# A graph network on one core: constants and scores of the gathering passes held in PSUM, small copies on ACT, and one bias matmul for three

## The chip, the core and the metric

The kernel runs on one NeuronCore of a Trainium2 chip. Its engines work side by side and meet only through semaphores: PE (TensorE, matrix products), ACT (ScalarE, functions and copies), DVE (VectorE, elementwise work), POOL (GpSimd, here mostly the issue of indirect gathers), and SP (SyncE, which issues the other DMAs). SBUF holds operands; PSUM, in banks of 2 KB per partition, holds what PE accumulates. The metric is the device time of one execution in microseconds; less is better.

## What is computed

A graph with 3125 nodes of 128 features and 100,000 edges, which come sorted by their destination `dst`, goes through four blocks, each applied to the relu of a layer norm of the node features `x` and added to them. The part that matters, in short:

```python
# block 1: three attention layers of the GAT kind over (src, dst)
# block 2: a message layer
m   = gelu(concat(h[dst], h[src], edge_attr) @ W1 + b1)
m   = gelu(m @ W2 + b2) @ W3 + b3
agg = segment_mean(m, dst)            # then an update of the node
# block 3: two layers of dynamic attention, 4 heads of 32 features
e     = leaky_relu(xl[src] + xr[dst], 0.2)
score = einsum('ehd,hd->eh', e, att)
mx    = segment_max(score, dst)
ex    = exp(score - mx[dst])
den   = segment_sum(ex, dst)
out   = segment_sum(ex / den[dst] * xl[src], dst)
# block 4: two convolution layers
out   = segment_sum(dinv[src] * edge_weight * dinv[dst] * (h @ W)[src], dst)
```

`segment_sum` adds the rows of all edges with the same destination.

## The kernel before

The nodes stand in 25 tiles of 128. The first block works densely: the number of edges between each pair of nodes is counted, and attention is taken over whole tiles. The other five passes (one message layer, two attention layers, two convolutions) are **gathering passes** over the edges. A plan cuts the sorted edges into 30 windows, each of which adds to one node tile; together they have 840 columns of 128 edges, in 220 chunks of at most four columns. Every gathering pass loops over windows, and inside over chunks.

`gather` (L1226) lets GpSimd issue one indirect DMA for each column: 128 rows of a table in HBM, chosen by `src`, land in SBUF as `g`. The message layer and the convolution have six such chunk buffers (`g1`), the attention layers 22 (`g2`), since they keep a window's rows until its scores are done.

Two one-hot matrices carry edges to nodes and back. `node_by_slot` (L1237) compares a row of node numbers, fetched by an SP DMA in bf16, with `pidx`, the number of the partition: `at`, nodes by edges. `slot_by_node` (L1242) compares `iota_row`, the numbers 0 to 127 along a row, with the local destination `dst_l`: `w`, edges by nodes. A segment sum is then a matmul of `w` with the rows, which accumulates in PSUM over all columns of a node tile. Every PSUM tile comes from one pool with two buffers for each name, `bank(name)`, each a whole bank; the accumulator is `bank("C")`, so that successive node tiles use two different banks.

In the message layer, for each chunk: the edge attributes are transposed on PE and copied out by DVE (`ets`, L1321); `by_feature` puts the sum of three bf16 parts of the destination's product times `at` (L1249), the edge part (L1332) and the transposed gathered rows (L1254) into one bank; ACT takes the gelu `x1` (L1338). Three bias matmuls with one row each (L1342) and four products with W2 (L1346) follow, the second gelu `x2` on ACT (L1349), a column of ones by GpSimd (L1351), the edge weights by DVE (L1352), and the accumulation (L1355).

In an attention layer, for each chunk of a window: `by_feature`; ACT and DVE take the leaky relu `low_y` (L1528, L1529); PE multiplies with the attention vector (L1532), and ACT copies the scores into `S` (L1534), a tile in SBUF. After the window, `run_maxima` finds the maximum of each run of edges with one destination by two scans along the columns and two along the partitions (L1455 to L1480); DVE subtracts it (L1538) and ACT takes the exponential (L1539). A second loop over the window's chunks multiplies the rows by it (`msg`, L1545), copies it beside them on ACT (L1548), builds `w` and accumulates (L1551).

In a convolution, for each column, `w` is compared and multiplied by the edge weight in one DVE instruction (L1603), and two passes of PE accumulate it (L1605).

Tiles are shared out by the framework, which sets a semaphore wait wherever an instruction touches what another engine's instruction still uses, and which lays the instructions of the loops out ahead of each other where buffers allow. Each engine then runs its own queue in order.

Of the kernel before, what the change touches and what calls it, by code (L numbers as in the profile page):

```python
# [18 lines left out]
P = 128  # L19
# [725 lines left out]
def sorted_path(ctx: ExitStack, tc: tile.TileContext, a: dict, out: bass.AP, flag_out: bass.AP):  # L745
# [20 lines left out]
    ps = ctx.enter_context(tc.tile_pool(name="f_ps", bufs=2, space=PSUM))  # L766
# [5 lines left out]
    def bank(name):  # L772
        return ps.tile([P, SL], F32, name=name)
# [118 lines left out]

    with tc.tile_pool(name="f_prep", bufs=1) as pp:
# [84 lines left out]
    wgt = ew_pool.tile([P, KT], F32, name="wgt")  # L978
# [6 lines left out]
    def load_edge_windows(pool):  # L985
        raw = pool.tile([P, KT], I32, name="raw", bufs=1)
        lo_r = pool.tile([P, KT], F32, name="lo_r", bufs=1)
        hi_r = pool.tile([P, KT], F32, name="hi_r", bufs=1)
        t_r = pool.tile([P, KT], F32, name="t_r", bufs=1)
        for i, (lo, hi, t, c0, k) in enumerate(plan.ew):  # L990
            cs = slice(c0, c0 + k)
            r = at_register(base_e, i, P * k)
            nc.sync.dma_start(src_i[:, cs], window_of(a["src"], r, k))
            nc.sync.dma_start(wgt[:, cs], window_of(a["edge_weight"], r, k))
            reads.append(nc.sync.dma_start(raw[:, cs], window_of(a["dst"], r, k)))
            nc.gpsimd.memset(lo_r[:, cs], float(lo))
            nc.gpsimd.memset(hi_r[:, cs], float(hi))
            nc.gpsimd.memset(t_r[:, cs], float(t * P))
        nc.vector.tensor_copy(dst_w, raw)

        nc.vector.tensor_tensor(lo_r, dst_w, lo_r, ALU.is_lt)
        nc.vector.tensor_tensor(hi_r, dst_w, hi_r, ALU.is_ge)
        nc.vector.tensor_add(lo_r, lo_r, hi_r)
        nc.vector.tensor_sub(dst_l, dst_w, t_r)
        nc.vector.scalar_tensor_tensor(dst_l, lo_r, FAR, dst_l, ALU.mult, ALU.add)
# [206 lines left out]
    for c0 in range(0, KT, P):  # L1212
        n = min(P, KT - c0)
        pt = bank("D")
        nc.tensor.transpose(pt[:n, :P], dst_l[:, c0:c0 + n], ident)
        t = wk.tile([P, P], BF16, name="place")
        nc.vector.tensor_copy(t[:n, :], pt[:n, :P])
        nc.sync.dma_start(place_d[c0:c0 + n, :], t[:n, :])

# [10 lines left out]
    def node_by_slot(c0, n):  # L1230

        row = wk.tile([P, SL], BF16, name="row", bufs=4)
        nc.sync.dma_start(row[:, :n * P], bass.AP(tensor=place_d.tensor,
                                                  offset=place_d.offset + c0 * P,
                                                  ap=[[0, P], [1, n * P]]))
        at = wk.tile([P, SL], BF16, name="at", bufs=3)
        nc.vector.tensor_scalar(at[:, :n * P], row[:, :n * P], pidx, None, ALU.is_equal)  # L1237
        return at

    def slot_by_node(c0, n):  # L1240
        w = wk.tile([P, C, P], F32, name="w", bufs=3)
        nc.vector.tensor_tensor(w[:, :n, :], bc(iota_row[:, None, :], [P, n, P]),  # L1242
                                bc(dst_l[:, c0:c0 + n, None], [P, n, P]), ALU.is_equal)
        return w
# [16 lines left out]
    def message_layer(H):  # L1261
# [8 lines left out]
        b2 = load_row("mb2", a["L1_gnn_mb2"], parts=1)  # L1270
# [9 lines left out]
        b2_3 = thirds(b2, "b2_", gp, D)  # L1280
# [8 lines left out]
        R3 = thirds(R, "R_", big, NT * D, "Z")  # L1289
        sums = big.tile([P, NT, D], F32, name="T")  # L1290
# [3 lines left out]
        for i, (lo, hi, t, w0, k) in enumerate(plan.ew):  # L1294
            if i == first_of[t]:
                acc = bank("C")
            r = at_register(base_e, i, P * k)
            ea = a["edge_attr_64"][bass.ds(r, P * k), :].rearrange("(p k) f -> p k f", p=P)
            for c0, n in chunks_of(w0, k):
# [10 lines left out]
                at = node_by_slot(c0, n)  # L1310

                et = bank("A")
# [28 lines left out]
                for q in range(3):  # L1341
                    nc.tensor.matmul(y2[:, :n * P], ones_bf[0:1, :],  # L1342
                                     bc(b2_3[q][:, None, :], [1, n, D]),
                                     start=(q == 0), stop=False, skip_group_check=True)
# [6 lines left out]
                nc.gpsimd.memset(x2[:, :n, D:D + 1], 1.0)  # L1351
                nc.vector.tensor_copy(x2[:, :n, D + 1:W], wgt[:, c0:c0 + n, None])  # L1352
                w = slot_by_node(c0, n)
# [38 lines left out]

    def find_runs(pool, keep):

        fwd = keep.tile([P, HEADS, KR], BF16, name="fwd")
        bwd = keep.tile([P, HEADS, KR], BF16, name="bwd")
# [15 lines left out]
        for h in range(HEADS):  # L1412
            nc.vector.tensor_scalar(fwd[:, h, :], one, -BIG, None, ALU.mult)
            nc.vector.tensor_scalar(bwd[:, h, :], other, -BIG, None, ALU.mult)
# [25 lines left out]

    def run_maxima(i, k, S):

        fwd = wk.tile([P, HEADS, k + 2], BF16, name="fw")
        bwd = wk.tile([P, HEADS, k + 2], BF16, name="bw")
        nc.vector.tensor_copy(fwd, breaks["fwd"][:, :, off[i]:off[i] + k + 2])
        nc.vector.tensor_copy(bwd, breaks["bwd"][:, :, off[i]:off[i] + k + 2])
# [5 lines left out]
        B = wk.tile([P, HEADS, k + 2], F32, name="B")  # L1452

        def scan():
            nc.vector.tensor_tensor_scan(flat(F), flat(fwd), flat(S), -BIG, ALU.add, ALU.max)  # L1455
            nc.vector.tensor_tensor_scan(flat(B)[:, ::-1], flat(bwd)[:, ::-1], flat(S)[:, ::-1], -BIG,
                                         ALU.add, ALU.max)
# [3 lines left out]
        pt = bank("D")  # L1461
        nc.tensor.matmul(pt[:HEADS, 0:P], F[:, :, k], ident, start=True, stop=True)
        nc.tensor.matmul(pt[:HEADS, P:2 * P], B[:, :, 1], ident, start=True, stop=True)
        edge = wk.tile([HEADS, 2 * P], F32, name="edge")
        nc.vector.tensor_copy(edge, pt[:HEADS, :2 * P])
# [3 lines left out]
        nc.vector.tensor_tensor_scan(run[:, 0, 1:], lane[:, :P], edge[:, :P], -BIG, ALU.add, ALU.max)  # L1469
        nc.vector.tensor_tensor_scan(run[:, 1, P - 1::-1], lane[:, :P - 1:-1], edge[:, :P - 1:-1], -BIG,  # L1470
                                     ALU.add, ALU.max)
        pt = bank("D")
# [11 lines left out]
    def dynamic_attention_layer(H, i_layer):  # L1484
# [13 lines left out]
        for h in range(HEADS):  # L1498
# [3 lines left out]
        HT = transposed(H, big.tile([P, NP], F32, name="T"))  # L1502
        T = big.tile([P, NT, D], F32, name="YT")
        product(HT, Wl, lambda t0, n, pt: nc.vector.tensor_add(
            T[:, t0:t0 + n, :], pt, bc(bl[:, None, :], [P, n, D])))
# [4 lines left out]
            bc(br[:, None, :], [P, n, D])))  # L1510
        R3 = thirds(R, "R_", big, NT * D, "T")
        Y = big.tile([P, NT, D], F32, name="Z")

        for i, (lo, hi, t, w0, k) in enumerate(plan.ew):
            if i == first_of[t]:
                acc = bank("C")
            gs = []
            S = wk.tile([P, HEADS, k + 2], F32, name="S")
            for c0, n in chunks_of(w0, k):
                j0 = c0 - w0  # L1520
                g = gp.tile([P, C, D], F32, name="g2", bufs=22)
                gs.append(g)
                gather(tab, g, 0, c0, n)
                at = node_by_slot(c0, n)
                y1 = bank("A")
                by_feature(y1, R3, t, at, g, 0, n)
                low_y = wk.tile([P, SL], F32, name="low_y", bufs=3)
                nc.scalar.mul(low_y[:, :n * P], y1[:, :n * P], SLOPE)  # L1528
                nc.vector.tensor_max(low_y[:, :n * P], y1[:, :n * P], low_y[:, :n * P])  # L1529
                sp = bank("B")  # L1530
                for c in range(n):
                    nc.tensor.matmul(sp[:, c * HEADS:(c + 1) * HEADS], low_y[:, c * P:(c + 1) * P], att_h,  # L1532
                                     start=True, stop=True)
                nc.scalar.copy(S[:, :, 1 + j0:1 + j0 + n].rearrange("p h c -> p c h"),  # L1534
                               sp[:, :n * HEADS].rearrange("p (c h) -> p c h", h=HEADS))
            M = run_maxima(i, k, S)
            ex = wk.tile([P, k, HEADS], F32, name="ex")
            nc.vector.tensor_sub(S[:, :, 1:k + 1], S[:, :, 1:k + 1], M[:, :, 1:k + 1])  # L1538
            nc.scalar.activation(ex.rearrange("p k h -> p h k"), S[:, :, 1:k + 1], AF.Exp)  # L1539
            for c0, n in chunks_of(w0, k):  # L1540
# [8 lines left out]
                w = slot_by_node(c0, n)  # L1549
# [25 lines left out]
    def convolution_layers(H):  # L1575
# [7 lines left out]
        for i_layer in (1, 2):  # L1583
# [9 lines left out]
            Y = big.tile([P, NT, D], F32, name="Z")  # L1593
            for i, (lo, hi, t, w0, k) in enumerate(plan.ew):
                if i == first_of[t]:
                    acc = bank("C")
                for c0, n in chunks_of(w0, k):
# [3 lines left out]
                    for c in range(n):  # L1601
                        j = c0 + c
                        nc.vector.tensor_scalar(w[:, c, :], iota_row, dst_l[:, j:j + 1], wgt[:, j:j + 1],  # L1603
# [17 lines left out]
    with tc.tile_pool(name="f_big1", bufs=1) as big, tc.tile_pool(name="f_w1", bufs=1) as wt, \  # L1621
            tc.tile_pool(name="f_g1", bufs=2) as gp:
        weights.append(wt)
        into_x(message_layer(prenorm("H")))
    with tc.tile_pool(name="f_big2", bufs=1) as big, tc.tile_pool(name="f_w2", bufs=1) as wt:
        weights.append(wt)
        with tc.tile_pool(name="f_runs", bufs=1) as rp:
            find_runs(rp, wt)
        h = prenorm("YT")
        with tc.tile_pool(name="f_g2", bufs=2) as gp:  # L1630
# [3 lines left out]
    with tc.tile_pool(name="f_big3", bufs=1) as big, tc.tile_pool(name="f_w3", bufs=1) as wt, \  # L1634
            tc.tile_pool(name="f_g3", bufs=2) as gp:
# [47 lines left out]
```

## Time and profile before

| what | value |
|---|---|
| median of 3 runs | 8938.41 us (8935.47 to 8966.12) |
| the profiled execution | 8952.42 us, span 8950.6 us |
| PE busy | 5047.8 us (56%) |
| weight loads (PEld) busy | 3996.2 us (45%) |
| DVE busy | 3410.2 us (38%) |
| ACT busy | 1265.6 us (14%) |
| POOL busy | 4110.5 us (46%) |

The profile is of one execution. Every engine's busy time is a share of the whole span, averaged over stages that differ; these can be told apart in the slices of the page:

```profile
PE   4677769999964455555635555555533333333332
...
POOL 1000036666624544444344444444266666566664
PEclk9999989999986677666666676666655555555555
```

Each digit is a fortieth of the span (224 us) in tenths. GpSimd becomes busy where the gathering passes begin: the message layer from about 1230 us, the attention layers from 2736 and 4590, the convolutions from 6457 and 7707. PEclk is the clock granted to PE.

### The profile page before, as it was taken

To read this page: it belongs to the slowest core of one execution; us is meant where nothing else is said; L and a number is where in the kernel's file an instruction comes from. 1 tells how busy PE (TensorE), PEld (TensorE's weight loads), DVE (VectorE), ACT (ScalarE), POOL (GpSimd) and SP (SyncE) were. 2 spreads that over 40 slices of the span, in tenths; PEclk is the share of its full clock that TensorE was granted. 3 is DMA by queue.
4 is the path that set the end of the run, shared out by engine and by line. 5 is a ranking of instruction groups with operands and counts; after the bars stand their busy time and mean duration, and the time that the engine had idled before them with its cause. 6 is when DMAs were issued, how large, how long until landed. Compare 5 with 4: busy or idle time off the path is not lost. (4 is left out here: it accounts for less than half of the span.)

```text
span 8950.6 us, 84054 instructions
## 1 busy us (share of the span) xinstructions
PE 5047.8 (56%) x28459; PEld 3996.2 (45%) x28744; DVE 3410.2 (38%) x8010; ACT 1265.6 (14%) x2766; POOL 4110.5 (46%) x5004
## 2 busy tenths in 40 slices
PE   4677769999964455555635555555533333333332
PEld 1267756666653444445534454444422332223222
DVE  8999942222243233333343333333522112212112
ACT  1644422222210011111101111111100000000000
POOL 1000036666624544444344444444266666566664
PEclk9999989999986677666666676666655555555555
DMA  1000022323211111111111111111111111111111
GB/s 26 7 3 1 1 59 84 84 84 84 81 40 48 49 48 50 46 47 47 44 42 45 48 49 46 48 46 48 31 45 47 46 46 46 44 45 47 46 46 41
DMA packets 311528, 411.33 MB, mean 46 GB/s; under 512 B 126095, under 2 KB 235070, under 8 KB 311093
## 3 DMA queue, kind: packets, MB, share of 16 engines
q0 software_dynamic: 134560, 276.34, 11.0%
q1 hardware_dynamic: 167379, 123.47, 5.1%
q10 hardware_dynamic: 9154, 6.03, 0.3%
q8 instruction: 236, 3.87, 0.2%
q14 instruction: 199, 1.63, 0.1%
HBM read 395.06 MB, written 10.44 MB: 45 GB/s over the span
## 5 line engine op out<-in xcount | busy, mean ns | idle before, releaser
L1226 POOL DMA_INDIRECT g<-tab,src_i x4200 | 4055.0, 965 | 3507.2 <-issue 1759.9
L1605 PE MATMUL C<-g,w 128*128 128x128 f32 x3360 | 897.1, 421 | 1513.7 <-issue 709.6
L1605 PEld LDWEIGHTS C<-g,w 128*128 128x128 f32 x3360 | 709.3, 298 | 1701.4 <-issue 1184.7
L1603 DVE TENSOR_SCALAR w<-iota_row,dst_l,wgt 128x128 f32<-128x128 f32 x1680 | 467.6, 361 | 1790.7 <-remote 1242.3
L1532 PE MATMUL B<-att_h,low_y 128*128 128x4 f32 x3360 | 541.4, 282 | 872.3 <-DVE low_y L1529 579.1
L1532 PEld LDWEIGHTS B<-att_h,low_y 128*128 128x128 f32 x3360 | 547.1, 244 | 911.4 <-DVE low_y L1529 604.0
L1254 PE MATMUL A<-ident,g 128*128 128x128 f32 x3360 | 672.7, 336 | 178.5 <-issue 165.2
L1254 PEld LDWEIGHTS A<-ident,g 128*128 128x128 f32 x3360 | 610.1, 243 | 279.2 <-issue 221.0
L1551 PE MATMUL C<-msg,w 128*128 128x132 f32 x3360 | 490.0, 301 | 410.5 <-DVE w L1242 206.4
L1551 PEld LDWEIGHTS C<-msg,w 128*128 128x128 f32 x3360 | 456.0, 210 | 439.2 <-issue 348.5
L1242 DVE TENSOR_TENSOR w<-iota_row,dst_l 128x512 f32<-128x512 f32 (+2 forms) x660 | 436.4, 664 | 524.8 <-remote 185.8
L1529 DVE TENSOR_TENSOR low_y<-A,low_y 128x512 f32<-128x512 f32 (+3 forms) x440 | 289.6, 662 | 680.2 <-ACT low_y L1528 484.8
L1249 PE MATMUL A<-at,R 128*128 128x512 bf16 (+3 forms) x1141 | 444.5, 461 | 79.1 <-issue 49.1
L1545 DVE TENSOR_TENSOR msg<-g,ex 128x512 f32<-128x512 f32 (+3 forms) x440 | 284.5, 669 | 523.2 <-issue 462.4
L1351 POOL MEMSET x<- 128x4 f32 (+1 forms) x220 | 26.6, 121 | 947.8 <-issue 929.8
L1528 ACT ACTIVATE low_y<-A 128x512 f32<-128x512 f32 (+3 forms) x440 | 252.3, 578 | 1378.7 <-remote 763.0
L1237 DVE TENSOR_SCALAR at<-row,pidx 128x512 bf16<-128x512 bf16 (+2 forms) x660 | 227.0, 349 | 452.8 <-remote 158.2
L867 ACT ACTIVATE T<-R 128x3200 f32<-128x3200 f32 x3 | 8.6, 2869 | 2492.1 <-DVE R L866 2492.1
L1321 DVE COPY ets<-A 128x256 f32<-128x256 f32 (+1 forms) x214 | 88.8, 415 | 620.7 <-PE A L1316 571.7
L1249 PEld LDWEIGHTS <-R 128*128 128x128 bf16 x1980 | 224.7, 125 | 173.0 <-issue 82.8
L1155 DVE SCALAR_TENSOR_TENSOR p<-up,s_src,dn 128x1024 f32<-128x1024 f32 (+1 forms) x225 | 294.2, 1321 | 4.0 <-PE C L1161 3.6
L1157 ACT ACTIVATE p<-p 128x1024 f32<-128x1024 f32 (+1 forms) x225 | 245.2, 1092 | 299.3 <-DVE p L1155 290.0
(350 smaller groups left out, 6688.0 us busy)
## 6 DMA issues: line engine op xcount, KB each, us to landing
row<-place_d SPq DMA_DIRECT2D x597, 128.0 KB
g<-tab,src_i POOLq DMA_INDIRECT x4200
er<-in_edge_attr_dram SPq DMA_DIRECT2D x39, 512.0 KB
tab<-T SPq DMA_DIRECT2D x3, 1600.0 KB
tab<-YT SPq DMA_DIRECT2D x2, 1600.0 KB
row<-place_d SPq DMA_DIRECT2D x24, 96.0 KB
out_dram<-X SPq DMA_DIRECT2D x1, 1536.0 KB
row<-place_d SPq DMA_DIRECT2D x21, 64.0 KB
```

Of the source, the lines that this page charges most:

```text
L1155: nc.vector.scalar_tensor_tensor(p[:, :n], up[:, :n], s_src[:, st:st + 1], dn[:, :n], ALU.add, ALU.max)
L1226: nc.gpsimd.indirect_dma_start(out=g[:, j0 + c, :], out_offset=None, in_=tab, in_offset=bass.IndirectOffsetOnAxis(ap=src_i[:, c0 + c:c0 + ...
L1242: nc.vector.tensor_tensor(w[:, :n, :], bc(iota_row[:, None, :], [P, n, P]), bc(dst_l[:, c0:c0 + n, None], [P, n, P]), ALU.is_equal)
L1249: nc.tensor.matmul(pt[:, :n * P], R3[i][:, t * D:(t + 1) * D], at[:, :n * P], start=(i == 0), stop=False, skip_group_check=True)
L1254: nc.tensor.matmul(pt[:, c * P:(c + 1) * P], g[:, j0 + c, :], ident, start=False, stop=(c == n - 1), skip_group_check=True)
L1528: nc.scalar.mul(low_y[:, :n * P], y1[:, :n * P], SLOPE)
L1529: nc.vector.tensor_max(low_y[:, :n * P], y1[:, :n * P], low_y[:, :n * P])
L1532: nc.tensor.matmul(sp[:, c * HEADS:(c + 1) * HEADS], low_y[:, c * P:(c + 1) * P], att_h, start=True, stop=True)
L1545: nc.vector.tensor_mul(msg[:, :n * HEADS, :HD], gs[j0 // C][:, :n, :].rearrange("p c (h d) -> p (c h) d", d=HD), bc(e[:, :, None], [P, n * ...
L1551: nc.tensor.matmul(acc[:, :AW], w[:, c, :], msg[:, c * HEADS:(c + 1) * HEADS, :].rearrange("p h d -> p (h d)"), start=(i == first_of[t] an ...
L1603: nc.vector.tensor_scalar(w[:, c, :], iota_row, dst_l[:, j:j + 1], wgt[:, j:j + 1], ALU.is_equal, ALU.mult)
L1605: nc.tensor.matmul(acc[:, :D], w[:, c, :], g[:, c, :], start=(i == first_of[t] and j == w0), stop=(i == last_of[t] and j == w0 + k - 1))
```

## The change

All of it lies in the gathering passes.

- `bank` takes a width and a number of buffers, and a pool of banks is opened for each block (`banks`). The one pool over all is gone.
- `still(width)` takes one bank "C" and puts four things into it: two accumulators (used in turn by node tiles), a copy of `iota_row` and a copy of `pidx`. `at` and every `w` read the constants from there. `at` becomes a `tensor_tensor` with a broadcast operand.
- In the message layer the three parts of the bias stand in three rows, so that one matmul with three rows adds them. The ones and the edge weights lie side by side in `one_wgt`, and one ACT copy puts both beside `x2`, in place of the GpSimd memset and the DVE copy.
- In the attention layers the scores `S` and the exponentials `ex` share a bank "S" (two buffers); the products with the attention vector and the small products of the run maxima share one bank "E" with one buffer; the backward scan writes to a bank "B". The masks `fwd` and `bwd` lie by window, so that the two copies of them for each window go; the copy `edge` goes, an ACT copy `firsts` comes. The difference of score and maximum is written to `M` in SBUF.

```diff
+    def bank(name, width=SL, bufs=2):
+        return pools[-1].tile([P, width], F32, name=name, bufs=bufs)
...
+    def still(width):
+        t = bank("C", bufs=1)
+        iota_ps, pidx_ps = t[:, 2 * width:2 * width + P], t[:, 2 * width + P:2 * width + P + 1]
+        nc.vector.tensor_copy(iota_ps, iota_row)
+        nc.vector.tensor_copy(pidx_ps, pidx)
+        return [t[:, :width], t[:, width:2 * width]], iota_ps, pidx_ps
...
-        nc.vector.tensor_scalar(at[:, :n * P], row[:, :n * P], pidx, None, ALU.is_equal)
+        nc.vector.tensor_tensor(at[:, :n * P], row[:, :n * P], bc(pidx_ps, [P, n * P]), ALU.is_equal)
...
-        nc.vector.tensor_tensor(w[:, :n, :], bc(iota_row[:, None, :], [P, n, P]),
+        nc.vector.tensor_tensor(w[:, :n, :], bc(iota_ps[:, None, :], [P, n, P]),
...
-                acc = bank("C")
+                acc = accs[t % 2]
...
-                for q in range(3):
-                    nc.tensor.matmul(y2[:, :n * P], ones_bf[0:1, :],
-                                     bc(b2_3[q][:, None, :], [1, n, D]),
-                                     start=(q == 0), stop=False, skip_group_check=True)
+                nc.tensor.matmul(y2[:, :n * P], ones_bf[0:3, :], bc(b2_s[:, None, :], [3, n, D]),
+                                 start=True, stop=False, skip_group_check=True)
...
-                nc.gpsimd.memset(x2[:, :n, D:D + 1], 1.0)
-                nc.vector.tensor_copy(x2[:, :n, D + 1:W], wgt[:, c0:c0 + n, None])
+                nc.scalar.copy(x2[:, :n, D:W], one_wgt[:, c0:c0 + n, :])
...
-        B = wk.tile([P, HEADS, k + 2], F32, name="B")
+        B = bank("B", 2 * P, 1)[:, :HEADS * (k + 2)].rearrange("p (h k) -> p h k", h=HEADS)
...
-        edge = wk.tile([HEADS, 2 * P], F32, name="edge")
-        nc.vector.tensor_copy(edge, pt[:HEADS, :2 * P])
+        firsts = wk.tile([P, HEADS], F32, name="firsts")
+        nc.scalar.copy(firsts, B[:, :, 1])
+        edge = small[:, :2 * P]
...
-            S = wk.tile([P, HEADS, k + 2], F32, name="S")
+            both = bank("S")
+            S = both[:, :HEADS * (k + 2)].rearrange("p (h k) -> p h k", h=HEADS)
...
-                sp = bank("B")
+                sp = small[:, 3 * P + turn % 2 * 64:3 * P + turn % 2 * 64 + 64]
...
-                        nc.vector.tensor_scalar(w[:, c, :], iota_row, dst_l[:, j:j + 1], wgt[:, j:j + 1],
+                        nc.vector.tensor_scalar(w[:, c, :], iota_ps, dst_l[:, j:j + 1], one_wgt[:, j, 1:2],
```

## The prediction

> **What bounds the kernel now.** I began with the page's busy shares, its slices of granted clock and its groups of instructions. No engine is full over the span, and the clock falls from 0.9 to 0.5 as the stages go by, so one bound for the whole cannot exist. Of the groups, these matter (busy time, mean of one, then the idle time before it and who ended it):
>
> ```profile
> L1226 POOL DMA_INDIRECT g<-tab,src_i x4200 | 4055.0, 965 | 3507.2 <-issue 1759.9
> ...
> L1603 DVE TENSOR_SCALAR w<-iota_row,dst_l,wgt 128x128 f32<-128x128 f32 x1680 | 467.6, 361 | 1790.7 <-remote 1242.3
> ...
> L1242 DVE TENSOR_TENSOR w<-iota_row,dst_l 128x512 f32<-128x512 f32 (+2 forms) x660 | 436.4, 664 | 524.8 <-remote 185.8
> ...
> L1237 DVE TENSOR_SCALAR at<-row,pidx 128x512 bf16<-128x512 bf16 (+2 forms) x660 | 227.0, 349 | 452.8 <-remote 158.2
> ```
>
> GpSimd issues 840 gathers in each of five passes. In the timeline they follow each other after 1.25 us (0.94 busy, 0.31 between), so a pass cannot take less than 840 x 1.25 = 1050 us. The chain that ended last names work for less than a third of the span:
>
> ```profile
> POOL 13%; issue 9%; another core or an unknown queue 2%; DVE 2%; DMA 2%; PE 1%; ACT 0%; POOLq 0%; ACTq 0%; SPq 0%
> ```
>
> So I read the stages. This is the view by windows, over each pass without its ends (length, then busy us of PE, weight load, VectorE, ACT, GpSimd, then clock and DMA):
>
> ```profile
> 1300.00:2500.00 1200.00, 1114.05 (x6822) 825.80 (x6918) 322.83 (x856) 247.59 (x397) 746.17 (x957) 0.99 0.30 84
> 2736.00:4449.00 1713.00, 925.97 (x5396) 793.60 (x5477) 528.48 (x1279) 197.77 (x633) 816.73 (x838) 0.66 0.17 48
> ...
> 6457.00:7651.00 1194.00, 446.02 (x1666) 353.56 (x1666) 244.52 (x862) 0.00 (x0) 787.42 (x832) 0.55 0.16 46
> ```
>
> The message layer is bound by PE (93% busy at full clock). The convolution takes 1194 us, 144 above the gather floor, with VectorE busy a fifth of the time: VectorE is not a bound by its work. The attention layers take 1713, 663 above the floor, and neither PE nor VectorE is full. Why is seen inside one node tile, in 5 us windows:
>
> ```profile
> 3740.00:3745.00 5.00, 2.29 (x10) 2.07 (x10) 0.00 (x0) 0.00 (x0) 3.78 (x5) 0.50 0.29 72
> 3745.00:3750.00 5.00, 0.84 (x2) 0.21 (x2) 0.00 (x0) 0.00 (x0) 3.78 (x5) 0.50 0.18 52
> ...
> 3765.00:3770.00 5.00, 4.78 (x22) 4.19 (x23) 1.06 (x5) 0.97 (x3) 0.00 (x0) 0.50 0.17 52
> 3770.00:3775.00 5.00, 5.00 (x22) 4.19 (x21) 1.05 (x3) 0.68 (x2) 0.00 (x0) 0.50 0.09 26
> ```
>
> While GpSimd gathers without a pause, PE issues one instruction in 1.4 us and nothing else runs; when GpSimd stops for want of buffers, PE is full at once. I call this the **crawl**. The timeline has VectorE idle through it:
>
> ```profile
> 3756.08 0.37 PE L1254 MATMUL A<-ident,g 128*128 128x128 f32 x1 [2.21 <-issue]
> ...
> 3758.90 0.32 DVE L1237 TENSOR_SCALAR at<-row,pidx 128x384 bf16<-128x384 bf16 x1 [20.32 <-PE A L1254]
> ```
>
> VectorE waited 20.32 us for PE. What slows PE I cannot name; VectorE's reads cannot be it, since it read nothing.
>
> **What the change does to each stage.** As built, the changed kernel carries a wait at every place where two engines touch the same 2 KB bank of PSUM, whatever columns they use. The bank "C" now holds both accumulators, the column indices and the node index. So 1630 of 1680 convolution `w` wait for the preceding accumulating matmul; before, most waited only for the buffer of three chunks ago. In the message layer `at` and `w` wait likewise. The Trainium skill says this of the hardware too ("PSUM — Partial Sum Buffer", § PSUM bank collisions raise a hardware error): engines must be kept apart by bank and quadrant, not by address.
>
> **Rule against row.** For the change speaks "SBUF — State Buffer", § Who interferes with whom: VectorE with two SBUF inputs, or in a fast two-port mode, locks the port pair that it shares with GpSimd; with one SBUF input it does not. The row: a gather takes 944 ns at the median and 965 in the mean. By the rule the remedy could be worth whatever gathers lose; by the row that is 4200 x 0.021 = 88 us at most, of which the attention passes hold (975-944) x 840 = 26 each. I take the row, and of it nothing, since gathers are late mainly for buffers. The price of the remedy: `at` at 349 ns becomes a tensor_tensor like L1242, 664.
>
> *Message layer.* A 4-column chunk repeats after 6.06 us (the bias matmuls start at 1801.73 and 1807.79). From the timeline:
>
> ```profile
> 1802.16 0.69 ACT L1338 ACTIVATE x<-B,mb 128x512 f32<-128x512 f32 x1 [3.39 <-PE B L1254]
> ...
> 1804.23 0.60 ACT L1349 ACTIVATE x<-D 128x512 f32<-128x512 f32 x1 [1.38 <-PE A L1316]
> ...
> 1804.85 0.35 DVE L1237 TENSOR_SCALAR at<-row,pidx 128x512 bf16<-128x512 bf16 x1 [0.22 <-issue]
> 1804.94 0.97 PEld L1355 LDWEIGHTS C<-x,w 128*128 128x128 f32 x8 [0.63 <-issue]
> ```
>
> Three bias matmuls (0.82) stand where PE waits for the first gelu (start 1802.16, W2 at 1802.89). One matmul saves 0.55 of PE's work but PE then waits: 0. The memset (0.12) and the weight copy (0.28) go, an ACT copy comes (0.2, like the 128x16 copies of L1548); it follows the second gelu, on the path. Now the loop: gelu 0.69 and signal 0.13; W2 matmuls 1.16 to the next start, 1.2; second gelu 0.60, copy 0.2, signals 0.28, 1.08; accumulating matmuls 0.9; only then `at`, 0.66 and signals, 1.1; then the three R matmuls 0.65, edge part 0.87, gathered part 0.9 and lag 0.6, 3.0. Sum 0.82+1.2+1.08+0.9+1.1+3.0 = **8.1 us**. Before, `at` ran beside the matmuls, and R3 before the accumulation. So +2.0 x 210 chunks = **+420** (250 if the edge part of the next chunk fills waits, 500 if not all signals are this short). GpSimd then rests 3 us of each 8, so no crawl. PE is busy 4.7 of 8.1 us; the clock stayed full elsewhere in this trace at such shares.
>
> *Convolution.* Per chunk 1190/210 = 5.67 us. In the timeline four `w` take 1.22 and eight matmuls 2.08, overlapping: about 2.4 us of work, 3.3 of waits. One by one, a column costs 0.34 + 0.52 + 0.1 = 0.96, a chunk 3.85. If the late answers of PE stay as they are, +1.45 x 210 = +305 per pass. If PE answers at once, 3.85 fits under the four gathers (5.0) and the pass falls to the floor: -140. Nearest is the row of `w` with "remote" 1242.3, PE signals that come late; but some of the 3.3 can absorb it. I take half the upper end, **+150** a pass, 300 in both.
>
> *Attention layers.* A tile takes 65 us (the 5 us windows: GpSimd busy to 3756, idle until 3790): 41 of gathers (33 x 1.25) and 24 of pause. Before, the messages of one window ran among the scores of the next. Now `at` of the next window waits for bank C until the last accumulation, so three phases come one after another. Scores: per chunk 2.6 us of PE at full clock, 5.2 at half; 3.3 taken, x 8.3 chunks = 27. Run maxima: first scan 3704.6 to the exponential's end 3712.6, 8, plus the copy and waits among shared banks, 11. Accumulation: msg 0.67, `w` 0.66 and matmuls 0.97, no longer overlapped, 2.3 x 8.3 = 19. Sum 57. Removed copies (0.19 twice, edge 0.41) are in it, under 1 us a tile. With no crawl: 57, -8 x 25 = -200. With the crawl hiding only the 10 us of PE that it hides now: 41 + 47 = 88, +575. The nearest row is the crawl; but 3713 to 3724 show PE full in the first 10 us of a gather run, and accumulation, which frees buffers, now falls there. So 16 of 57 hidden, 41 + 41 = 82 at worst, and 73 where a run is broken up: I take +8 x 25 = **+200** a layer, 400 in both.
>
> Other stages: the start (0 to 1220) is dense attention and keeps its banks: 0. Sum +420 +300 +400 = +1120 on the profiled run's 8952.42 (span 8950.6) gives 10072; the median of the runs is 14 lower, so **10050**.
>
> **Rivals.**
> *Only the message layer pays* (0.25): waits in the gather-limited passes absorb the serial loop. 8938 + 420 = 9360. For it: VectorE is idle most of both passes. Against: idle for PE's late signals.
> *Faster* (0.17), one mechanism: the crawl comes from GpSimd's share of a port after all, so with PSUM operands PE answers at once. Then convolution -140 x 2, attention at 50 us a tile, -15 x 25 x 2 = -750, message +420: 8330; with only half of it 8650. It decides when an attention tile takes under 59 us. For it: the crawl appears only while GpSimd gathers. Against: VectorE idle in it.
> *The clock falls* (0.10): if 4.7 of 8.1 us is too little, PE's part doubles: 4.7 more x 210 = 990 on top, 11050.
> *The forecast* 0.45, own range 9600 to 10600; 0.03 is left to accidental balance.
>
> A difference of 0.5% is about what this measurement can tell from none. Faster 0.17, same 0.03, slower 0.80. The range from 8700 to 10900 leaves out half the fast case and most of the clock case.
>
> **What would show it.** Message layer: chunks 8.1 us apart, `at` idle until PE's C. Convolution: `w` waiting for PE C in every column. Attention: no score work between accumulations, and a crawl still there. A crawl gone, with GpSimd's idle time small, makes this wrong.

## The result, and the profile after

The changed kernel takes 9925.24 us (median of 4 runs, 9909.29 to 9931.19), the kernel before, beside it, 8943.58: a ratio of 1.109 (95% interval 1.1066 to 1.1115). It is slower, as forecast, and 125 us below the forecast time. The profiled execution has a span of 9923.7 us, 973 more than before. Counted from the first gather of a pass to the first of the next (the last to the end of the span), the traces give:

| us | message layer | attention 1 | attention 2 | convolution 1 | convolution 2 |
|---|---|---|---|---|---|
| before | 1506 | 1854 | 1867 | 1250 | 1255 |
| after | 1717 | 2176 | 2191 | 1307 | 1311 |
| difference | +211 | +322 | +324 | +57 | +57 |

The first 1220 us are the same. So the loss lies in all five passes, two thirds of it in the attention layers. The groups of the page after:

```profile
L1248 POOL DMA_INDIRECT g<-tab,src_i x4200 | 3986.2, 949 | 5487.9 <-issue 3234.6
...
L1635 DVE TENSOR_SCALAR w<-C,dst_l,one_wgt 128x128 f32<-128x128 f32 x1680 | 687.4, 409 | 1765.1 <-issue 848.5
L1264 DVE TENSOR_TENSOR w<-C,dst_l 128x512 f32<-128x512 f32 (+2 forms) x660 | 437.8, 663 | 1547.7 <-remote 1058.9
L1259 DVE TENSOR_TENSOR at<-row,C 128x512 bf16<-128x512 bf16 (+2 forms) x660 | 425.8, 660 | 1060.1 <-PE C L1380 593.6
```

A gather's mean falls from 965 to 949 ns: 69 us less work for GpSimd over 4200 gathers, which then waits 1980 us more than before (5487.9 against 3507.2). The last line names the wait that came: `at` stands 593.6 us for PE's accumulation in C. By windows, over the same passes:

```profile
1300.00:2700.00 1400.00, 1054.85 (x6462) 835.53 (x6554) 339.56 (x663) 265.81 (x598) 717.76 (x762) 0.99 0.28 72
2950.00:4890.00 1940.00, 994.06 (x5267) 845.88 (x5335) 599.58 (x1175) 194.02 (x645) 786.03 (x834) 0.61 0.17 41
7310.00:8530.00 1220.00, 648.54 (x1630) 408.40 (x1630) 339.49 (x839) 0.00 (x0) 784.72 (x832) 0.50 0.18 45
```

In the message layer PE is now busy 75% of the time in place of 93%, still at full clock. One turn of its loop, in the timeline:

```profile
1801.08 0.69 ACT L1366 ACTIVATE x<-B,mb 128x512 f32<-128x512 f32 x1 [4.51 <-PE B L1276]
...
1803.02 0.60 ACT L1375 ACTIVATE x<-D 128x512 f32<-128x512 f32 x1 [1.25 <-PE D L1372]
...
1803.67 1.16 PE L1380 MATMUL C<-x,w 128*128 128x130 f32 x8 [0.69 <-ACT x L1375]
...
1804.87 0.69 DVE L1259 TENSOR_TENSOR at<-row,C 128x512 bf16<-128x512 bf16 x1 [4.25 <-PE C L1380]
...
1805.61 0.81 PE L1271 MATMUL B<-at,R 128*128 128x512 bf16 x2 [0.46 <-DVE at L1259]
...
1808.21 0.69 ACT L1366 ACTIVATE x<-B,mb 128x512 f32<-128x512 f32 x1 [4.51 <-PE B L1276]
```

Each step is released by the one above it: a ring of one gelu, W2, the other gelu, accumulation, `at`, R. It closes after 7.13 us, and 210 chunks of +1.07 make +225.

In an attention layer the three phases of a tile now follow each other, and the accumulation runs in the crawl. The timeline of one tile's accumulation, with the wait before each `w` in brackets; "remote" is what the profile writes where no instruction ended just before the wait did:

```profile
3584.88 0.69 DVE L1264 TENSOR_TENSOR w<-C,dst_l 128x512 f32<-128x512 f32 x1 [2.49 <-PE C L1582]
...
3585.72 2.10 PE L1582 MATMUL C<-msg,w 128*128 128x132 f32 x8 [1.68 <-DVE w L1264]
...
3597.54 0.69 DVE L1264 TENSOR_TENSOR w<-C,dst_l 128x512 f32<-128x512 f32 x1 [11.37 <-remote]
...
3598.37 2.10 PE L1582 MATMUL C<-msg,w 128*128 128x132 f32 x8 [10.56 <-issue]
...
3616.46 0.69 DVE L1264 TENSOR_TENSOR w<-C,dst_l 128x512 f32<-128x512 f32 x1 [17.64 <-remote]
```

GpSimd gathers from 3573.4 to 3613.1 without a pause. The first chunks take 3 us, the later ones 12 and 19, and 3 us after the last gather the speed is back. The lines of PE show what is late here: eight matmuls take 2.10 us, as they did before the crawl, and end, as the profile reckons it, at 3587.82 and 3600.47; the next `w`, which waits for nothing else, starts 9.7 and 16.0 us later. In this tile it is PE's signal that comes late, not its work.

### The profile page after: what moved, and what is told of

Its sections match the earlier page's. It is cut to its first block, busy times and chain, and to the rows that moved or that the text cites. A ratio compares the mean times of both kernels' runs of the same rounds, so it can differ in the third digit from the quotient of the medians.

```text
span 9923.7 us, 82168 instructions
## 1 busy us (share of the span) xinstructions
PE 5667.2 (57%) x28045; PEld 4328.4 (44%) x28304; DVE 3836.2 (39%) x7617; ACT 1300.9 (13%) x3106; POOL 4015.7 (40%) x4784
## 5 line engine op out<-in xcount | busy, mean ns | idle before, releaser
L1248 POOL DMA_INDIRECT g<-tab,src_i x4200 | 3986.2, 949 | 5487.9 <-issue 3234.6
L1637 PE MATMUL C<-g,w 128*128 128x128 f32 x3360 | 1336.8, 501 | 1190.0 <-DVE w L1635 649.4
L1582 PE MATMUL C<-msg,w 128*128 128x132 f32 x3360 | 889.7, 445 | 1445.5 <-DVE w L1264 957.3
L1582 PEld LDWEIGHTS C<-msg,w 128*128 128x128 f32 x3360 | 765.7, 330 | 1556.3 <-issue 1354.5
L1635 DVE TENSOR_SCALAR w<-C,dst_l,one_wgt 128x128 f32<-128x128 f32 x1680 | 687.4, 409 | 1765.1 <-issue 848.5
L1264 DVE TENSOR_TENSOR w<-C,dst_l 128x512 f32<-128x512 f32 (+2 forms) x660 | 437.8, 663 | 1547.7 <-remote 1058.9
L1259 DVE TENSOR_TENSOR at<-row,C 128x512 bf16<-128x512 bf16 (+2 forms) x660 | 425.8, 660 | 1060.1 <-PE C L1380 593.6
L1563 PE MATMUL E<-att_h,low_y 128*128 128x4 f32 x3360 | 443.1, 254 | 257.1 <-issue 134.4
L1563 PEld LDWEIGHTS E<-att_h,low_y 128*128 128x128 f32 x3360 | 442.8, 205 | 270.4 <-issue 135.5
L1380 PE MATMUL C<-x,w 128*128 128x130 f32 x1680 | 248.9, 290 | 164.1 <-ACT x L1375 158.6
L1576 DVE TENSOR_TENSOR msg<-g,S 128x512 f32<-128x512 f32 (+3 forms) x440 | 288.9, 657 | 55.0 <-ACT msg L1579 29.8
```

Of the source, the lines that this page charges most:

```text
L1248: nc.gpsimd.indirect_dma_start(out=g[:, j0 + c, :], out_offset=None, in_=tab, in_offset=bass.IndirectOffsetOnAxis(ap=src_i[:, c0 + c:c0 + ...
L1259: nc.vector.tensor_tensor(at[:, :n * P], row[:, :n * P], bc(pidx_ps, [P, n * P]), ALU.is_equal)
L1264: nc.vector.tensor_tensor(w[:, :n, :], bc(iota_ps[:, None, :], [P, n, P]), bc(dst_l[:, c0:c0 + n, None], [P, n, P]), ALU.is_equal)
L1380: nc.tensor.matmul(acc[:, :W], w[:, c, :], x2[:, c, :], start=(i == first_of[t] and j + c == 0), stop=(i == last_of[t] and j + c == k - 1))
L1582: nc.tensor.matmul(acc[:, :AW], w[:, c, :], msg[:, c * HEADS:(c + 1) * HEADS, :].rearrange("p h d -> p (h d)"), start=(i == first_of[t] an ...
L1635: nc.vector.tensor_scalar(w[:, c, :], iota_ps, dst_l[:, j:j + 1], one_wgt[:, j, 1:2], ALU.is_equal, ALU.mult)
```

## The experiments

All ratios are to the kernel before, run beside each set on the same chip (its medians there were 8866.51, 8871.54 and 8960.97 us). Stage times come from one profile each; those of different sets differ by up to 2.3% for equal code (an attention layer 1854 and 1812), so I use them for differences of 50 us and more.

**Constants in a bank of their own.**

```diff
         t = bank("C", bufs=1)
-        iota_ps, pidx_ps = t[:, 2 * width:2 * width + P], t[:, 2 * width + P:2 * width + P + 1]
+        k = bank("K", bufs=1)
+        iota_ps, pidx_ps = k[:, :P], k[:, P:P + 1]
```

> The changed kernel, with the column indices and the node index in a PSUM bank of their own, apart from the accumulators. Theory (VectorE and PE take turns on the one bank C): the message layer falls from 7.13 us a chunk to about 6.1 (stage about -210 us), the w of a convolution no longer wait for each column, and in the attention layers scores and messages of two windows interleave again: 9000 to 9200 us. Rival 1 (operands in PSUM, or the order of instructions, cost by themselves): 9800 to 9950. Rival 2 (the banks of the scores and of the run maxima keep the windows of the attention layers apart): the message layer recovers, the attention layers stay at about 2180 us each, 9600 to 9700.

9481.91 us, 1.0711 (1.0674 to 1.0748): in none of the three ranges. The message layer falls to 1576 and the convolutions to 1243 and 1252, but the attention layers stay at 2068 and 2117, and not by the rival's banks of scores, as the next run shows. Only VectorE reads bank K, and yet every `at` of the next window still stands behind every `w` of this one, in VectorE's own queue:

```profile
3548.49 0.42 DVE L1265 TENSOR_TENSOR w<-K,dst_l 128x256 f32<-128x256 f32 x1 [1.96 <-remote]
...
3549.16 1.28 DVE L1260 TENSOR_TENSOR at<-row,K 128x512 bf16<-128x512 bf16 x2
3570.95 0.16 DVE L1590 TENSOR_SCALAR rd<-C 128x4 f32<-128x4 f32 x1 [20.51 <-remote]
...
3571.03 0.68 DVE L1260 TENSOR_TENSOR at<-row,K 128x512 bf16<-128x512 bf16 x1
```

The first `w` line is the last of its window. Two `at` of the next window follow it; then `rd`, which reads the tile's sums, stands 20.51 us for the end of the accumulation, and the third `at` comes behind it. In the program all `w` of a window precede `at` of the next. As built, the users of one PSUM bank keep that order even on one engine: in the runs below where `at` and `w` do not share a bank, VectorE's queue mixes them.

**Constants from SBUF**, all else as changed.

```diff
-        return [t[:, :width], t[:, width:2 * width]], iota_ps, pidx_ps
+        return [t[:, :width], t[:, width:2 * width]], iota_row, pidx
...
-        nc.vector.tensor_tensor(at[:, :n * P], row[:, :n * P], bc(pidx_ps, [P, n * P]), ALU.is_equal)
+        nc.vector.tensor_scalar(at[:, :n * P], row[:, :n * P], pidx, None, ALU.is_equal)
```

> The changed kernel, with the constants read from SBUF as before (at again a tensor_scalar), all else as changed: both accumulators in one bank, scores in PSUM, one bias matmul, ACT copies. Theory (sharing of bank C): like the kernel with the constants in their own bank, 9000 to 9200, at 0.3 us shorter where VectorE is waited for. If operands in PSUM bring anything against GpSimd's port, this one is the slower of the two; if they cost, the faster. Rival (banks of the scores): 9600 to 9700, as there.

8745.22 us, 0.9878 (0.9838 to 0.9918): 1.2% faster than before, and faster than I expected. So the rest of the change (scores and scan in PSUM, two accumulators in one bank, fewer copies, one bias matmul) costs nothing and gains 1.2%, in the attention layers (1761 and 1780); which of its parts brings that was not separated. The whole loss hangs on where two constants lie.

**One constant at a time.** Three runs put one of the two into PSUM and leave the other in SBUF. The first two use a bank of their own, the third the accumulators' bank:

> The changed kernel with the column indices in a PSUM bank of their own and the node index in SBUF (at a tensor_scalar as before). As built, at and w then share no bank, and VectorE's queue mixes the windows of an attention layer as it does with all constants in SBUF. Theory (the common bank ties at and w to program order, and that is what the kernel with one bank for both constants still paid): within 0.5% of the kernel with constants in SBUF, 0.983 to 0.993 of the kernel before. Rival (a PSUM operand costs by itself): 1.05 or more. A gain from GpSimd's port would show as less than 0.98.

> The other half: the node index in a PSUM bank of its own (at a tensor_tensor of 0.66 us in place of 0.35), the column indices in SBUF. Theory: again near the kernel with constants in SBUF, with 0.31 us more in each of 660 at, of which only part is on a path: 0.985 to 1.005 of before. Rival (reading PSUM costs, or at's length): 1.03 or more.

> The changed kernel with the column indices in the accumulators' bank as changed, but the node index in SBUF. Theory: at is free, so the attention layers' windows mix and the message layer's at runs ahead again; but w waits for each accumulation. Message layer 6.1 to 6.6 us a chunk (w was built a chunk ahead before), convolutions as in the changed kernel (1307 us with their ends), attention layers between 1780 and 2100: 1.00 to 1.06 of before. If most of the changed kernel's loss were the turns on bank C, and not the order of at and w, this would stay at 1.08 to 1.11.

| | message | attention 1, 2 | convolution 1, 2 | ratio (95%) |
|---|---|---|---|---|
| `w` from its own bank | 1510 | 1775, 1800 | 1245, 1250 | 0.9903 (0.987 to 0.9935) |
| `at` from its own bank | 1484 | 1833, 1832 | 1247, 1247 | 0.9995 (0.9976 to 1.0014) |
| `w` from bank C | 1516 | 1687, 1723 | 1301, 1303 | 0.9863 (0.983 to 0.9895) |

A PSUM operand by itself costs nothing in `w`, and gains nothing against 0.9878 with SBUF. With `at` from PSUM the kernel is about 1% longer. The longer `at` may be why (0.31 us in each of 220 is 68 us a layer, and the attention layers are 72 and 52 longer than with SBUF), but the order of VectorE's queue differs between these runs as well, and that share is not separated. The third line I had wrong: `w` takes turns with the accumulation on bank C, and this costs the convolutions 55 us each, as expected, but the attention layers not at all, as long as `at` is free. They are even 74 and 57 us shorter than with all constants in SBUF; these runs do not show why.

**The counterpart: `at` in bank C, `w` in SBUF.**

```diff
-        nc.vector.tensor_tensor(w[:, :n, :], bc(iota_ps[:, None, :], [P, n, P]),
+        nc.vector.tensor_tensor(w[:, :n, :], bc(iota_row[:, None, :], [P, n, P]),
```

and the same in the convolution's `w`.

> The changed kernel with only the node index in the accumulators' bank, the column indices in SBUF: the counterpart of the run with w in that bank. As built, at of a window stands behind the last accumulation of the window before. Theory (the loss is at, which a common bank puts behind the accumulation; w's turns cost only the convolutions 55 us each): message layer and attention layers within 3% of the changed kernel's (1717, 2176, 2191), convolutions as before (1250): 1.08 to 1.10 of before. Rival (w's turns and at's place must come together): 1.03 or less.

9585.55 us, 1.0709 (1.0657 to 1.076), a little under the range: message layer 1713 (all of its loss), attention layers 2048 and 2078 (most of theirs, but 5 to 6% under the changed kernel's, where I expected 3% at most), convolutions 1251 and 1256. Against `at` from its own bank, which differs in the bank alone, this is 7%. What remains to the changed kernel (1.109) is `w` in C too: about 110 us in the convolutions and 128 and 113 in attention layers where `at` is already held.

**Three attempts on the crawl.** First, three gather buffers for six in the convolutions (`name="g1", bufs=3`):

> The kernel before, with three gather buffers in place of six in the two convolutions. The traces show PE's late answers beginning some 20 gathers into a run without a pause. Theory (an uninterrupted run of gathers brings the crawl): with room for 12 columns no run gets that long before PE answers, and a convolution falls from about 1220 to 1080 to 1120 us each: 8720 to 8800 in all. Rival (PE is late whenever GpSimd gathers, and fewer buffers only make GpSimd wait more): a convolution rises to 1300 or more, 9100 and up.

8866.33 us, 1.0 (0.9984 to 1.0017): neither; the convolutions stay at 1242 and 1247, and GpSimd still finds stretches of over 30 us without a pause (the longest 34.8). But the waits changed. Most of what `w` waited for before was "remote" (1242.3 us in the row that the prediction shows); now an instruction of PE has ended just before:

```profile
L1603 DVE TENSOR_SCALAR w<-iota_row,dst_l,wgt 128x128 f32<-128x128 f32 x1680 | 478.9, 362 | 1773.5 <-PE C L1605 1331.9
```

So most of the late signals are gone (in the first convolution `w` waits 148.0 us for "remote", before 655.2) and the time is the same. GpSimd now waits there 114.6 us for PE to free a buffer, where it waited 17.3; its "remote" waits fell from 147.5 to 55.4. What was gained on one side was lost on the other.

Second, a small memset after each gather (`nc.gpsimd.memset(pace, 0.0)`):

> The kernel before, with a small GpSimd memset (128x4, 0.12 us busy) after every gather. A gather then takes 1.4 to 1.6 us in place of 1.25, so the floor of a pass rises to 1180 to 1340 us. Theory (the gathers are issued faster than something behind them takes them, and the backlog starves PE): the crawl goes, the attention layers fall from 1712 to about 1350 a pass, the convolutions stay near 1200 to 1350, the message layer gains or loses little: 8200 to 8700. Rival (only real idleness of GpSimd lets PE go on): each pass rises by 150 to 300 us, 9500 and up.

8969.8 us, 1.012 (1.0085 to 1.0156). This tells nothing of the crawl, because the memsets are not where I put them. The slices of this kernel's page show GpSimd busy from the start, in the dense stage:

```profile
POOL 7776006666653444544534545454166666566664
```

They depend on nothing and went ahead; the first gather of the message layer is 112 us later than before, and the passes are unchanged.

Third, a memset that cannot be moved, since the gathers write what it clears, in all passes:

```diff
     def gather(tab, g, j0, c0, n):
+        nc.gpsimd.memset(g[:, j0:j0 + n, :], 0.0)
```

> The kernel before, with GpSimd clearing each chunk's gather buffer (memset of up to 128x512) before its gathers, so that a pause of some tenths of a microsecond to 2 us stands between every four gathers; this cannot be moved ahead, as the small memset of the last trial was. Theory (uninterrupted gathers starve PE): a pause in each chunk ends the crawl as in the message layer before, the convolutions come to 1050 + 210 x the pause, and the attention layers fall below 1500: 0.92 to 0.98 of before. Rival (only idleness by lack of buffers lets PE go on, or GpSimd's activity as such holds PE): 1.02 to 1.15.

8466.38 us, 0.9534 (0.9502 to 0.9567). Half of it came as expected: the attention layers fall to 1605 and 1604, not below 1500, with 0.52 us of extra work for GpSimd in every chunk. Profiles of the same layers without the pause give 1812 to 1867, so a layer gains some 210 to 260 us, and the order of ACT's instructions in them is the same in both kernels. The convolutions do not move (1252, 1254), although GpSimd does about 105 us more work in each: the pause costs there about what it brings. The message layer loses about 40.

**The pause on the kernel with constants in SBUF**, in the attention layers alone, once and twice:

```diff
                 g = gp.tile([P, C, D], F32, name="g2", bufs=22)
                 gs.append(g)
+                nc.gpsimd.memset(g[:, :n, :], 0.0)
+                nc.gpsimd.memset(g[:, :n, :], 0.0)
```

> The changed kernel with its constants in SBUF, and with GpSimd clearing each gather buffer (0.52 us) before its gathers in the attention layers alone. If the two gains are of different origin they add: 0.988 x the attention layers' part of the cleared kernel (250 us each less, so 0.945): 0.93 to 0.95 of before. If both are the same gain (gathers that start later): 0.95 to 0.98.

> As the last, with two such clearings, a pause of about 1.05 us in each four gathers as in the message layer before. If a longer pause ends the crawl altogether: attention layers at 1350 to 1450 with their ends, 0.90 to 0.93 of before. If one clearing has already brought what there is: no better than that run, or worse by up to 115 us a layer.

Once: 8738.37 us, 0.9754 (0.971 to 0.9798), with attention layers at 1750 and 1756: the two gains do not add, and the number lies in the range of the second reading. Twice: **8156.11 us, 0.9109** (0.9067 to 0.9151), with 1445 and 1476. This beats both kernels. Its first attention layer by windows, over the gathers of the layer, and then two windows of 5 us inside it (length, then busy PE, weight load, VectorE, ACT, GpSimd, and clock):

```profile
2720.00:4030.00 1310.00, 966.87 (x5507) 833.41 (x5592) 543.12 (x1231) 190.16 (x674) 996.53 (x1238) 0.74 0.25 62
```

```profile
3520.00:3525.00 5.00, 5.00 (x20) 4.11 (x21) 3.02 (x12) 0.60 (x1) 3.78 (x5) 0.50 0.28 69
3525.00:3530.00 5.00, 5.00 (x22) 4.44 (x23) 0.12 (x1) 0.31 (x2) 4.08 (x6) 0.50 0.32 83
```

In these two windows PE is full while GpSimd gathers, at the same half clock at which it stood still before; over the 100 us from 3500 it is busy 81%. GpSimd is now busy 996.53 of 1310 us: the pass is near its new floor (1050 and 220 x 1.05 make 1281).

Is it the pause? The waits of `w` for late signals in the first attention layer, with none, one and two clearings (us, times, longest):

```profile
DVE w L1261 <- remote: 364.7, 44, 16.2
DVE w L1261 <- remote: 180.6, 37, 13.5
DVE w L1261 <- remote: 57.2, 18, 5.1
```

They shrink with the pause. But the three runs differ in more: with one clearing ACT's instructions in the attention layers stand in the same order as with none, with two they do not. So how much of the gain with two is the pause, and how much the other order, is not shown.

**A quarter of the gathers**, on the kernel before: only the first column of each chunk is gathered, the others are zeros.

> The kernel before with the gather buffers cleared and only the first column of each chunk gathered, so that three quarters of the gathers are left out and the sums use zeros for them. What a pass costs without the gather floor and without long runs of gathers. If gathers bring the crawl: attention layers at 1000 to 1200 us with their ends (PE's 926 us of busy time at 0.66 of the clock, less as the clock rises), convolutions below 800. If PE is late for another reason: attention layers above 1500, convolutions above 1000.

5249.71 us, 0.5857 (0.5831 to 0.5883). The attention layers take 879 and 904, less than I expected, the convolutions 436 and 437, the message layer 1372. The two lines of its page show PE full and at nearly full clock through the attention layers:

```profile
PE   3666878777999999998399999949999965664663
...
PEclk9899999998999999999699999969999987998997
```

So gathers hold PE back: without most of them PE does the same matmuls in half the time. This run leaves out the gathers' time itself, which has a floor of 1050 us; what the crawl adds to an attention layer is at most the difference between that floor and 1712, since waits for buffers are in it too.

## Why the prediction was right, and where it was not

Direction and size were right, and so was the mechanism: constants in the accumulators' bank put `at` and `w` behind the accumulation. That the sum (+1120) came so near to +973 is in part luck: its three terms, +420, +400 and +300, measured +211, +646 and +114.

*Message layer, +420 forecast, +211 measured.* The ring was the right one, with `at` behind the accumulation, and 8.1 us was too long by 0.97. Mis-sized terms: second gelu and copy, 1.08 forecast and 0.65 measured from gelu to accumulation, since the copy's end barely follows the gelu's; `at` and its signals, 1.1 and 0.74 (1804.87 to 1805.61); R, edge and gathered parts, 3.0 forecast and 2.60 measured (1805.61 to 1808.21). The accumulation went the other way, 0.9 and 1.20. The bias matmuls and the copies together were worth nothing, as said: with the constants in SBUF the layer takes 1496, and in two runs of the kernel before that leave its work there unchanged, 1493 and 1498.

*Attention layers, +200 a layer forecast, +323 measured.* That the windows would stop mixing was right; the cause was right by half. The step "`at` of the next window waits for bank C until the last accumulation" holds, but a bank with no other engine in it (1.0711) did the same to `at`, through the order of VectorE's queue. The sizes were off both ways: scores 27 us forecast for 8.3 chunks, 20 measured for 7 (3623.0 to 3643.2), so about 24; maxima 11, 5.7 measured (3566.3 to 3572.0); accumulation 19, 50 measured (3572.0 to 3622.4, 8 chunks), since gathers run through it and the crawl begins after 12 us. The accumulation is the term that was mis-sized most; the forecast came near all the same, because it had counted the crawl elsewhere, as gathers that hide only 16 of the 57 us. A tile takes 1955/25 = 78 us, between the 73 taken and the 82 named "at worst".

*Convolution, +150 a pass forecast, +57 measured.* The loop by column is there:

```profile
7603.20 0.41 DVE L1635 TENSOR_SCALAR w<-C,dst_l,one_wgt 128x128 f32<-128x128 f32 x1 [0.89 <-PE C L1637]
...
7603.66 0.80 PE L1637 MATMUL C<-g,w 128*128 128x128 f32 x2 [0.51 <-DVE w L1635]
7604.50 0.41 DVE L1635 TENSOR_SCALAR w<-C,dst_l,one_wgt 128x128 f32<-128x128 f32 x1 [0.89 <-PE C L1637]
```

It closes in 1.30 us, not 0.96: `w` from PSUM takes 0.41 for 0.34, and PE answers after 0.80 at half clock. That is just above a gather's 1.25, and so most of the loss hides behind the gathers: 840 x 1.30 = 1092, and `w` waits 150.5 us more for late signals in the first convolution, which comes near the 1231 from its first gather to its last. The column was taken too short and the share that the waits absorb too small; the two errors offset each other in part.

*Rule against row.* The row decided rightly. Gathers did get shorter (965 to 949 ns), and it is `w` that does it: the mean is 949 to 951 ns in all four runs with `w` from PSUM and 964 to 972 in the runs with `w` from SBUF and all gathers. That agrees with the direction of the rule in the Trainium skill. The prediction left out one limit in its section ("SBUF — State Buffer", § Who interferes with whom): two SBUF inputs count only against a GpSimd instruction that reads SBUF. Still `w` from PSUM in its own bank gained nothing over SBUF (0.9903 against 0.9878, intervals overlapping).

*The rivals.* "Only the message layer pays" was nearer to the truth of the convolutions than my sum. The fast rival failed on its own sign, an attention tile under 59 us: a tile takes 78, and the crawl is still there after, with VectorE's operands in PSUM. (With half of its gains, 515, and the whole cost of the message layer its second sum is 8843, not 8650.) "The clock falls" failed too: the clock of the message layer stayed at 0.99.

## What to carry to other kernels

Where a framework keeps PSUM's users in order by bank, a constant in PSUM ties every instruction that reads it to every other user of the bank, in program order; give it a bank whose users already come in that order, or leave it in SBUF. When a change loses, put back one operand at a time: here seven placements of two constants spanned 0.99 to 1.11. A gain in one engine's instruction (a shorter gather) is worth nothing while that engine waits for buffers, and a pause in its stream can be worth more.

## What the runs showed of the hardware that was not expected

While GpSimd issues gathers without a pause, PE's answers come late. In the three stretches read here this begins some 8 to 14 us into a run of gathers in the attention layers (before and after) and 23 us into one in a changed convolution, and it is over within some microseconds of the last gather. It has two faces. In the changed kernel PE's matmuls run at their usual pace and only the signals that they are done are late, by 9.7 and 16.0 us in the tile above. In the kernel before, PE's own instructions also come in steps of 1.4 or 2.8 us. There the trace has no event of PE's semaphore from 3737.09 to 3758.87, while PE issues on, and then eight of them within 0.36 us (3761.03 to 3761.39), as if they had stood in a queue.

One pause of 0.52 us in each four gathers took some 210 to 260 us off an attention layer in one kernel and next to nothing in another (11 and 24); two of them, with a changed order of instructions, took some 310 off there. In the convolutions one pause cost what it brought. What it is between the gathers and PE that holds the signals back is not shown by these runs: VectorE and ACT were idle meanwhile, the gather itself is not longer, and the DMA engines were busy about a fifth of the time. Whether a longer pause helps the convolutions was not tried.
